# Neighbour lists without MATCH_REPLACE8, and layer 1's NaN step fused with the residual's addition

## The chip, the cores and the metric

The kernel runs on one core of one Trainium2 chip. The metric is the time of one execution on the device in microseconds (us), the median of several runs. Names of engines as in the profile: PE is TensorE, DVE is VectorE, ACT is ScalarE, POOL is GpSimd, SP is SyncE, which only starts transfers.

## The reference

Sixteen graphs of 1024 nodes with 64 features go through four layers. Every layer takes `h = relu(layernorm(x))` and adds its result to `x`. The adjacency matrix is 1024 x 1024 per graph, symmetric in where it is not zero, with some 16 neighbours per node.

```python
# layer 0: messages = adj @ h; x += tanh([h, messages] @ W1 + b1) @ W2 + b2
# layer 1:
A = edges + jnp.eye(N)
num = jnp.einsum('bij,bjd->bid', A, nodes)
denom = jnp.sum(A, axis=2, keepdims=True)
out = num / denom
x = x + jnp.where(jnp.isnan(out), 0, out)
# layer 2: thin out the neighbours of each node by rank, then, over those that remain,
adj_d = _dilate_adj(adj, mask)
agg = _weighted_nanquantile_agg(h, adj_d > 0)   # per feature: sort the neighbours' values,
                                                # 0.25*q(0.25) + 0.5*q(0.5) + 0.25*q(0.75)
x = x + (relu((h + agg) @ W1 + b1) @ W2 + b2) * mask
# layer 3: x += (adj @ h / rowsum) @ W_neighbors + h @ W_self + bias
```

Layer 2 is the dear one: for every node the values of its neighbours have to be gathered and sorted, in each of the 64 features.

## The kernel before

One program works on all graphs. Six streams (adjacency, layers, tail, gathers, lists, sorts) are Python generators; while the program is built, a simple model of the engines' clocks (`clk`) decides which stream emits its next instructions, so the order of each engine's instructions is fixed at build time. `clk.dve += 1.2` and the like are that model's durations; they do nothing on the chip but shape the order.

For layer 2, each node's row of keys is made by TensorE and ScalarE: at column j the key is 1024 - j for a neighbour that remains and 0 elsewhere, in f16. Nodes are ordered by their number of neighbours, so that 128 nodes (one per partition) with similar counts share a group. A group has a cap on the neighbours: 38, 20, 18, 16, 13, the last three for two times 128 nodes each. The lists stream gathers the rows of keys and takes the largest eight keys at a time. MAX8 finds the eight largest; MATCH_REPLACE8 (with a MATCH_VALUE_LOAD ahead of it) then puts 0 in their places, so that the next MAX8 finds the next eight:

```python
found = lists.tile([P, total], F16, name="found", bufs=1)
for b0, n, cap, _ in GROUPS:       # (0,1,38,..), (1,1,20,..), (2,2,18,..), (4,2,16,..), (6,2,13,..)
    for i in range(b0, b0 + n):
        src, at = ks[i]
        yield at
        for r in range(-(-cap // 8)):
            e = found[:, o:o + 8]
            nc.vector.max(out=e, in_=src)                                        # L1034
            clk.dve += 1.2
            if (r + 1) * 8 < cap:
                nc.vector.match_replace(out=src, in_to_replace=e, in_values=src, imm_value=0.0)  # L1037
                clk.dve += 1.3
            o += 8
            yield clk.dve
        load_keys(i + KB)          # an indirect DMA by GpSimd, L1017
index = lists.tile([P, total], I32, name="index")
ts(index, found, -1.0, float(N), op0=ALU.mult, op1=ALU.add)                      # L1043
```

GpSimd then gathers the neighbours' feature rows, one indirect DMA for each place of the list (L1154), into one buffer per group, `raw`. VectorE sorts each group with a network of minima and maxima between two buffers, `raw` and `other` (L1197), and adds up the weighted places in `agg` (L1220). `agg` goes to DRAM and comes back in the nodes' own order as `res` (L1240). A group of the next graph can be gathered only when this graph's group is sorted, as there is one `raw` per group. The node order itself is one column block `node` (L1002).

Large tensor_scalar operations elsewhere, for comparison: `gone` (L930) compares 1024 f16 values with a pointer scalar, a number per partition read from memory.

Layer 1 divides and then puts 0 for a NaN, by adding the maximum with 0 and the minimum with 0[...]. Then it adds to `x`:

```python
ts(den, p[:, :, C:C + 1], 1.0, None, op0=ALU.add)                # L1118
nc.vector.reciprocal(den, den)
o, o1 = mid(0, [P, NB, C]), mid(0, [P, NB, C])
tt(o, p[:, :, :C], ha[:, :, :C], ALU.add)                        # L1121
tt(o, o, den.to_broadcast([P, NB, C]), ALU.mult)                 # L1122
ts(o1, o, 0.0, None, op0=ALU.max)                                # L1124
ts(o, o, 0.0, None, op0=ALU.min)                                 # L1125
tt(o, o, o1, ALU.add)                                            # L1126
tt(x, x, o, ALU.add)                                             # L1127
clk.dve += 3.8
```

`ts` is tensor_scalar and `tt` tensor_tensor, both on VectorE. `den` comes from 32 matmuls of messages (L843) and ScalarE's copy of them (L844).

Of the kernel before, what the change touches and what calls it, by code (L numbers as in the profile page):

```python
# [7 lines left out]
F32 = mybir.dt.float32  # L8
F16 = mybir.dt.float16
BF = mybir.dt.bfloat16  # L10
I32 = mybir.dt.int32
U16 = mybir.dt.uint16
U8 = mybir.dt.uint8
AF = mybir.ActivationFunctionType
ALU = mybir.AluOpType
AX = mybir.AxisListType

P = 128
C = 64
NB = 8  # L20
# [10 lines left out]
B_SW, B_SW2, B_LB, B_END = 0, 252, 504, 3576  # L31
H_ID, H_OFF, H_ONE, H_G, H_PI, H_END = 0, 128, 256, 384, 516, 1028

GROUPS = [(0, 1, 38, 17), (1, 1, 20, 15), (2, 2, 18, 12), (4, 2, 16, 10), (6, 2, 13, 1)]

E_ID, E_ONE, E_CAP, E_LOW, E_CN, E_Q, E_END = 0, 128, 256, 264, 272, 280, 320
J_ID, J_BIG, J_OFF, J_ST, J_ROW, J_ONE, J_PI, J_NI, J_END = 0, 128, 256, 384, 1408, 2432, 2560, 2688, 2696
KB = 4  # L40


# [665 lines left out]
def direct_path(ctx: ExitStack, tc: tile.TileContext, t: dict, out: bass.AP, flag):  # L708
# [24 lines left out]
    identf, onesf = cf[:, E_ID:E_ID + P], cf[:, E_ONE:E_ONE + P]  # L733
    cap8, low8, cn8 = (cf[:, e:e + NB] for e in (E_CAP, E_LOW, E_CN))
    identh, big_i, offdiag = (ch[:, e:e + P] for e in (J_ID, J_BIG, J_OFF))
    stair, pidx = ch[:, J_ST:J_ST + N], ch[:, J_PI:J_PI + P]
    nid = ch[:, J_NI:J_NI + NB]
    jrow, onerow = ch[0:1, J_ROW:J_ROW + N], ch[0:1, J_ONE:J_ONE + P]
    eps = const.tile([P, 1], F32, name="eps")
# [65 lines left out]
    def mid(u, shape):  # L805

        return work.tile(shape, F32, tag=f"mid{u}", name="mid", bufs=2)
# [200 lines left out]
    def neighbour_lists(b):  # L1008


        g = state[b]
        ks = []

        def load_keys(i):
            if i < NB:
                k = lists.tile([P, N], F16, name="k", bufs=KB)
                nc.gpsimd.indirect_dma_start(k, None, g["keys_d"],  # L1017
                                             bass.IndirectOffsetOnAxis(ap=g["node"][:, i:i + 1], axis=0))
                clk.pool = max(clk.pool, clk.dve) + 1.3
                ks.append((k, clk.pool + 3.5))  # L1020

        for i in range(KB):
            load_keys(i)
        total = sum(n * -(-cap // 8) * 8 for _, n, cap, _ in GROUPS)
        found = lists.tile([P, total], F16, name="found", bufs=1)
        m = g["m"]
        o = 0
        for b0, n, cap, _ in GROUPS:
            for i in range(b0, b0 + n):
                src, at = ks[i]  # L1030
                yield at
                for r in range(-(-cap // 8)):
                    e = found[:, o:o + 8]
                    nc.vector.max(out=e, in_=src)  # L1034
                    clk.dve += 1.2
                    if (r + 1) * 8 < cap:
                        nc.vector.match_replace(out=src, in_to_replace=e, in_values=src, imm_value=0.0)  # L1037
                        clk.dve += 1.3
                    o += 8
                    yield clk.dve  # L1040
                load_keys(i + KB)
        index = lists.tile([P, total], I32, name="index")
        ts(index, found, -1.0, float(N), op0=ALU.mult, op1=ALU.add)  # L1043

        s = nodes.tile([P, 2, NB], F32, name="s")
        tt(s[:, 0], m, cap8, ALU.is_gt)
        tt(s[:, 1], m, low8, ALU.is_lt)
        tt(s[:, 0], s[:, 0], s[:, 1], ALU.max)
        tt(bad, bad, s[:, 0], ALU.max)

        at = nodes.tile([P, 3, NB], F32, name="at")
        for k in range(3):
            ts(at[:, k], m, (k + 1) / 4, -(k + 1) / 4, op0=ALU.mult, op1=ALU.add)
        far = lists.tile([P, 3, QT], F32, name="far", bufs=1)
        o = 0
        for b0, n, cap, low in GROUPS:
            lo, hi = _span(cap, low)
            k = hi + 1 - lo
            tt(far[:, :, o:o + k * n].rearrange("p t (q i) -> p t q i", i=n),
               cf[:, None, E_Q + lo:E_Q + hi + 1, None].to_broadcast([P, 3, k, n]),  # L1060
               at[:, :, None, b0:b0 + n].to_broadcast([P, 3, k, n]), ALU.subtract)
            o += k * n
        act(far, far, AF.Abs)
        for k, w in enumerate((0.25, 0.5, 0.25)):
            act(far[:, k], far[:, k], AF.Relu, bias=wcol[:, k:k + 1], scale=-w)
        g.update(index=index)
        done.add(("index", b))
        yield after(1.7, act=1.7)
        wts = lists.tile([P, QT], F32, name="wts", bufs=3)
        tt(wts, far[:, 0], far[:, 2], ALU.add)  # L1070
        tt(wts, wts, far[:, 1], ALU.add)
        clk.dve += 0.4
        g.update(wts=wts)
        done.add(("lists", b))


    def layers(b):
        g = state[b]
        adjt = g["adjt"]
        x = nodes.tile([P, NB, C], F32, name="x", bufs=3)  # L1080
        nc.sync.dma_start(x, x_in[b].rearrange("(i p) c -> p i c", p=P))
        yield max(g["at"], clk.dve + 3)
        ha = nodes.tile([P, NB, C + 1], F32, name="ha")
        yield from preln(0, x, ha)
        zt = big(0, [P, N])
        transposed(ha, zt[:C])
        messages(ha, adjt, zt[C:], C)
        tt(x, x, b02, ALU.add)
        yield after(0.7, pe=10.5, act=1.1)
        th = big(0, [C, N])  # L1090
        for q in range(2):
            p = bank()
            nc.tensor.matmul(p[:C, :], w01, zt[:, q * 512:(q + 1) * 512], start=True, stop=True)
            act(th[:, q * 512:(q + 1) * 512], p[:C, :], AF.Tanh, bias=b01)
        dh = per_node(bank(), th, w02)
        yield after(0, pe=1.3, act=2.8) + 2.8
        tt(x, x, dh, ALU.add)
        clk.dve += 0.7
        ha = nodes.tile([P, NB, C + 1], F32, name="ha")
        yield from preln(0, x, ha)  # L1100

        nc.vector.memset(ha[:, :, C:], 1.0)  # L1102
        nt = big(0, [C + 1, N])
        messages(ha, adjt, nt, 0, C + 1)
        p = bank2().rearrange("p (i m) -> p i m", m=P)
        for i in range(NB):
            nc.tensor.transpose(p[:, i, :C + 1], nt[:, i * P:(i + 1) * P], identf[:C + 1, :C + 1])

        adjt_d = dram.tile([NB, P, N], F32, name="adjt_d", bufs=5)
        deg = nodes.tile([P, 3, NB], F32, name="deg", bufs=5)  # L1110
        for j in range(NB):
            act(adjt[:, j], adjt[:, j], AF.Copy, accum_out=deg[:, 0, j:j + 1])  # L1112
            nc.sync.dma_start(adjt_d[j], adjt[:, j])
        done.add(("adjt", b))
        yield after(0, pe=10.5, act=1.1) + 2.5
        clk.act += 10
        den = nodes.tile([P, NB, 1], F32, name="den")
        ts(den, p[:, :, C:C + 1], 1.0, None, op0=ALU.add)  # L1118
        nc.vector.reciprocal(den, den)
        o, o1 = mid(0, [P, NB, C]), mid(0, [P, NB, C])  # L1120
        tt(o, p[:, :, :C], ha[:, :, :C], ALU.add)  # L1121
        tt(o, o, den.to_broadcast([P, NB, C]), ALU.mult)  # L1122

        ts(o1, o, 0.0, None, op0=ALU.max)  # L1124
        ts(o, o, 0.0, None, op0=ALU.min)  # L1125
        tt(o, o, o1, ALU.add)  # L1126
        tt(x, x, o, ALU.add)  # L1127
        clk.dve += 3.8
        ha = nodes.tile([P, NB, C + 1], F32, name="h2", bufs=3)
        yield from preln(0, x, ha)  # L1130
        nc.sync.dma_start(h_ds[b % 3][:N].rearrange("(i p) c -> p i c", p=P), ha[:, :, :C])
        ts(deg[:, 1], deg[:, 0], 0.0, None, op0=ALU.is_equal)
        tt(deg[:, 0], deg[:, 0], deg[:, 1], ALU.add)
        ts(deg[:, 1], deg[:, 1], -1.0, 1.0, op0=ALU.mult, op1=ALU.add)
        nc.vector.reciprocal(deg[:, 2], deg[:, 0])
        tt(deg[:, 2], deg[:, 2], deg[:, 1], ALU.mult)
        clk.dve += 0.6
        g.update(x=x, h2=ha, inv_deg=deg[:, 2], adjt_d=adjt_d, rows_at=clk.dve + 4)
        done.add(("layers", b))
# [226 lines left out]
def _constants():  # L1366

    import numpy as np

    p = np.arange(P)  # L1370
    ef = np.zeros((P, E_END), np.float32)
    ef[p, E_ID + p] = 1
    ef[:, E_ONE:E_ONE + P] = 1
    for b0, n, cap, low in GROUPS:
        ef[:, E_CAP + b0:E_CAP + b0 + n] = cap
        ef[:, E_LOW + b0:E_LOW + b0 + n] = low
    ef[:, E_CN:E_CN + NB] = 512 * N + N - 1 - (p[:, None] + P * np.arange(NB))
    ef[:, E_Q:E_END] = np.arange(E_END - E_Q)
    eh = np.zeros((P, J_END), np.float32)
    eh[p, J_ID + p] = 1  # L1380
    eh[p, J_BIG + p] = 2048
    eh[:, J_OFF:J_OFF + P] = 1
    eh[p, J_OFF + p] = 0
    eh[:, J_ST:J_ST + N] = p[:, None] < np.arange(N)
    eh[p, J_ST + p] = 2050
    eh[0, J_ROW:J_ROW + N] = -1024 - np.arange(N)
    eh[0, J_ONE:J_ONE + P] = 1
    eh[:, J_PI:J_PI + P] = p
    eh[:, J_NI:J_NI + NB] = p[:, None] + P * np.arange(NB)
    return {**_general_constants(), "ef": ef, "eh": eh.astype(np.float16)}  # L1390
# [73 lines left out]
```

## Time and profile before

| what | us |
|---|---|
| time, median of 3 runs | 4112.07 (4109.65 to 4116.42) |
| span of the profiled execution | 5044.8 |
| VectorE busy | 3624.5 |
| GpSimd busy | 2863.8 |
| TensorE busy, matmuls | 2152.3 |
| ScalarE busy | 1413.3 |
| MATCH_REPLACE8, 224 times | 270.7 |
| MATCH_VALUE_LOAD, 224 times | 20.6 |

The profiled execution is longer than the timed ones; sizes are read from it, and the time from the runs. In a row of the costliest groups stand the line, the engine, the operation, the output and the inputs with partitions x elements and type, then the number of instructions, the busy time in us and the mean duration of one in ns, and at the end the idle time of the engine just ahead of them with what ended it. In the view in order of time, the columns are the start in us, the duration in us, then the same.

### The profile page before, as it was taken

The numbers are of one execution on the slowest core, as the hardware profiler recorded it, in microseconds if no ns is written. First come the engines' busy times: TensorE is split into PE (matmuls) and PEld (weight loads), VectorE is DVE, ScalarE is ACT, GpSimd is POOL, SyncE is SP. The second block draws the span as 40 slices with busy tenths as digits, with TensorE's granted clock in tenths as the row PEclk, the third lists the DMA queues.
The fourth block names the chain that finished last, engine by engine and source line by source line (L and its number), as shares of the span: only waits on it lengthen the run. The fifth ranks groups of instructions, "written<-read, shape, count | busy, mean of one in ns | idle before, by whom it ended". The sixth has DMA issues, their size and how long they took to land.

```text
span 5044.8 us, 33983 instructions
## 1 busy us (share of the span) xinstructions
PE 2152.3 (43%) x8387; PEld 1001.3 (20%) x8387; DVE 3624.5 (72%) x9482; ACT 1413.3 (28%) x2594; POOL 2863.8 (57%) x2707
## 2 busy tenths in 40 slices
PE   6442414444345442454444444543445454343222
PEld 3211102121121211212121121212122121211011
DVE  2535685776678568688786868877786887768975
ACT  6332312242232421224232223323232232421000
POOL 0426366364575446756666666655676575466770
PEclk8655656666667665676666667665667666566555
DMA  3313323243242423424343343423334342333331
GB/s 107 66 60 73 62 59 52 63 98 64 77 74 63 119 35 83 66 64 111 60 105 68 97 66 87 82 56 97 70 97 74 83 81 56 79 70 78 55 55 43
DMA packets 251857, 372.70 MB, mean 74 GB/s; under 512 B 120160, under 2 KB 120352, under 8 KB 251648
## 3 DMA queue, kind: packets, MB, share of 16 engines
q0 software_dynamic: 92640, 117.88, 20.0%
q1 hardware_dynamic: 158864, 251.87, 15.1%
q8 instruction: 68, 1.11, 0.1%
q14 instruction: 141, 1.16, 0.1%
q10 hardware_dynamic: 144, 0.69, 0.0%
HBM read 256.97 MB, written 113.25 MB: 73 GB/s over the span
## 4 chain that ended last, share of the span: by engine, by line
DVE 49%; another core or an unknown queue 20%; PE 10%; issue 10%; ACT 7%; POOL 2%; DMA 2%; SPq 0%; ACTq 0%; DVEq 0%; POOLq 0%
DVE other L1197 13%; DVE raw L1197 12%; DVE found L1034 5%; DVE k L1037 4%; DVE agg L1220 4%; PE pt L843 4%; ACT adjt L1112 1%; POOL raw L1154 1%; PE pt L849 1%; DVE half L1220 1%; ACT nb L954 1%; PE tm L1284 1%; DVE nb L872 1%; ACT pt L956 1%
## 5 line engine op out<-in xcount | busy, mean ns | idle before, releaser
L1154 POOL DMA_INDIRECT raw<-h_d,index x2432 | 2554.3, 1050 | 1098.7 <-issue 722.6
L1197 DVE TENSOR_TENSOR other<-raw 128x128 f32<-128x128 f32 (+7 forms) x1488 | 763.6, 532 | 101.5 <-remote 59.4
L1197 DVE TENSOR_TENSOR raw<-other 128x256 f32<-128x256 f32 (+10 forms) x1424 | 676.5, 488 | 17.5 <-DVE other L1197 10.0
L843 PE MATMUL pt<-adjt,ha 128*65 128x512 f32 (+1 forms) x1024 | 496.5, 647 | 220.4 <-DVE ha L1102 220.3
L1017 POOL DMA_INDIRECT k<-keys_d,node x128 | 139.1, 1086 | 749.6 <-DVE node L1002 575.6
L879 PE MATMUL pt<-ef,a 128*128 128x128 f32 x1024 | 247.6, 409 | 677.3 <-ACT adjt L880 505.1
L1284 PE MATMUL tm<-at,ha 128*64 128x512 f32 x512 | 321.4, 742 | 430.2 <-issue 219.2
L954 ACT ACTIVATE nb<-pt 128x1024 f16<-128x1024 f32 x128 | 130.9, 1023 | 1123.3 <-remote 681.6
L1034 DVE MAX8 found<-k 128x8 f16<-128x1024 f16 x352 | 424.1, 1221 | 13.5 <-DVE k L1037 4.2
L920 PE MATMUL pt<-eh,nbt 128*128 128x512 f16 (+3 forms) x1024 | 221.7, 378 | 256.2 <-ACT nbt L909 157.9
L879 PEld LDWEIGHTS pt<-ef,a 128*128 128x128 f32 x1024 | 182.6, 212 | 736.4 <-ACT adjt L880 538.5
L1240 POOL DMA_INDIRECT res<-agg_d,pos x128 | 161.5, 1262 | 270.7 <-DMA agg_d<-agg 131.9
L1037 DVE MATCH_REPLACE8 k<-found,k 128x1024 f16<-128x1024 f16 x224 | 270.7, 1209 | 0.0
L843 PEld LDWEIGHTS pt<-adjt,ha 128*65 128x65 f32 (+1 forms) x1024 | 150.4, 151 | 546.3 <-issue 546.1
L1197 DVE TENSOR_TENSOR raw<-other,raw 128x128 f32<-128x128 f32 (+5 forms) x560 | 194.2, 354 | 86.2 <-remote 68.2
L1197 DVE TENSOR_TENSOR other<-raw,other 128x256 f32<-128x256 f32 (+4 forms) x592 | 206.4, 353 | 62.6 <-remote 43.3
L885 ACT ACTIVATE nb<-nb 128x512 f16<-128x512 f16 x256 | 159.5, 627 | 272.4 <-DVE nb L872 117.7
L945 PE MATMUL pt<-nb,eh 128*128 128x512 f16 x256 | 124.3, 485 | 210.3 <-ACT pt L956 132.8
L925 ACT ACTIVATE ab<-pt,sf 128x512 f16<-128x512 f32 x256 | 162.9, 693 | 175.4 <-remote 64.7
L1197 DVE TENSOR_TENSOR raw<-raw,other 128x256 f32<-128x256 f32 (+3 forms) x608 | 201.6, 336 | 0.0
L832 PE MATMUL pt<-ef,res 128*64 128x128 f32 x128 | 30.5, 418 | 393.5 <-DVE res L1244 304.3
L844 ACT COPY big<-pt 64x1024 f32<-64x1024 f32 (+1 forms) x32 | 32.2, 1008 | 583.4 <-PE pt L843 321.9
(154 smaller groups left out, 3998.9 us busy)
## 6 DMA issues: line engine op xcount, KB each, us to landing
a<-in_adj_dram SPq DMA_DIRECT2D x128, 512.0 KB
adjt_d<-adjt SPq DMA_DIRECT2D x128, 512.0 KB
at<-adjt_d SPq DMA_DIRECT2D x256, 256.0 KB
raw<-h_d,index POOLq DMA_INDIRECT x2432
keys_d<-nb SPq DMA_DIRECT2D x128, 256.0 KB
x<-in_x_dram SPq DMA_DIRECT2D x16, 256.0 KB
h_d<-h SPq DMA_DIRECT2D x16, 256.0 KB
agg_d<-agg SPq DMA_DIRECT2D x16, 256.0 KB
```

What stands on the lines that cost most here:

```text
L843: nc.tensor.matmul(p[p0:p0 + n, s], h[:, j, :n], adjt[:, j, s], start=j == 0, stop=j == NB - 1)
L879: nc.tensor.transpose(p[:, u * P:(u + 1) * P], a[:, j * P:(j + 1) * P], identf)
L920: nc.tensor.matmul(p[:, o:e], nbt[:, j, :], stair[:, :e - o], start=j % 4 == 0, stop=j % 4 == 3)
L925: act(ab[:, s], p[:, s], AF.Abs, bias=sf[:, 2 + q, i:i + 1], scale=2.0)
L954: act(nb[:, i, :], p, AF.Relu)
L1034: nc.vector.max(out=e, in_=src)
L1037: nc.vector.match_replace(out=src, in_to_replace=e, in_values=src, imm_value=0.0)
L1154: nc.gpsimd.indirect_dma_start(raw[:, s, i * C:(i + 1) * C], None, h_ds[b % 3], bass.IndirectOffsetOnAxis(ap=g["index"][:, at:at + 1], axi ...
L1197: tt(to, v0, v1, ALU.max if greater else ALU.min)
L1220: nc.vector.scalar_tensor_tensor(to, v, wq, to, op0=ALU.mult, op1=ALU.add)
L1240: nc.gpsimd.indirect_dma_start(res[:, i, :], None, g["agg_d"], bass.IndirectOffsetOnAxis(ap=g["pos"][:, i:i + 1], axis=0))
L1284: nc.tensor.matmul(p[:C, :], ha[:, j, :C], ats[k], start=j == 0, stop=j == NB - 1)
```

## The change

The lists no longer use MATCH_REPLACE8. After the first eight, the least key found so far is subtracted from every key, in place, as 16-bit whole numbers. What has been found already is then 0 or more; what has not is below 0. Read as 16-bit numbers without sign, the numbers below 0 are the largest, and the largest of them is the next key below the least. So MAX8 over that view gives the next eight, and a small tensor_scalar on eight numbers (the minimum with 0, plus the least key) makes keys of them again. In further rounds the large tensor_scalar adds the old least key and subtracts the new one in one pass. `found` is now f32[...].

Layer 1's four last operations become two: the maximum with 0 added to `x`, and the minimum with 0 added to `x`. The table `stair` has half its columns, of which the rest was not read; the model's durations are set anew.

```diff
-        found = lists.tile([P, total], F16, name="found", bufs=1)
+        found = lists.tile([P, total], F32, name="found", bufs=1)
...
-                for r in range(-(-cap // 8)):
-                    e = found[:, o:o + 8]
-                    nc.vector.max(out=e, in_=src)
-                    clk.dve += 1.2
-                    if (r + 1) * 8 < cap:
-                        nc.vector.match_replace(out=src, in_to_replace=e, in_values=src, imm_value=0.0)
-                        clk.dve += 1.3
+                nc.vector.max(out=found[:, o:o + 8], in_=src)
+                clk.dve += 1.15
+                yield clk.dve
+                less, before = src.bitcast(I16), None
+                for r in range(1, -(-cap // 8)):
+                    least = found[:, o + 7:o + 8]
+                    if r == 1:
+                        ts(less, src, least, None, op0=ALU.subtract)
+                    else:
+                        ts(less, less, before, least, op0=ALU.add, op1=ALU.subtract)
+                    before = least
+                    most = nodes.tile([P, 8], U16, name="most")
+                    nc.vector.max(out=most, in_=less.bitcast(U16))
                     o += 8
+                    ts(found[:, o:o + 8], most.bitcast(I16), 0.0, least, op0=ALU.min, op1=ALU.add)
+                    clk.dve += 1.8
                     yield clk.dve
+                o += 8
                 load_keys(i + KB)
...
-        o, o1 = mid(0, [P, NB, C]), mid(0, [P, NB, C])
+        o = mid(0, [P, NB, C])
         tt(o, p[:, :, :C], ha[:, :, :C], ALU.add)
         tt(o, o, den.to_broadcast([P, NB, C]), ALU.mult)
-        ts(o1, o, 0.0, None, op0=ALU.max)
-        ts(o, o, 0.0, None, op0=ALU.min)
-        tt(o, o, o1, ALU.add)
-        tt(x, x, o, ALU.add)
-        clk.dve += 3.8
+        nc.vector.scalar_tensor_tensor(x, o, 0.0, x, op0=ALU.max, op1=ALU.add)
+        nc.vector.scalar_tensor_tensor(x, o, 0.0, x, op0=ALU.min, op1=ALU.add)
+        clk.dve += 2.4
...
-    eh[:, J_ST:J_ST + N] = p[:, None] < np.arange(N)
+    eh[:, J_ST:J_ST + N // 2] = p[:, None] < np.arange(N // 2)
```

More of the change, by code (lines that the diff above doesn't have):

```diff
@@ L32 @@
 H_ID, H_OFF, H_ONE, H_G, H_PI, H_END = 0, 128, 256, 384, 516, 1028
+I16 = mybir.dt.int16
 GROUPS = [(0, 1, 38, 17), (1, 1, 20, 15), (2, 2, 18, 12), (4, 2, 16, 10), (6, 2, 13, 1)]
 E_ID, E_ONE, E_CAP, E_LOW, E_CN, E_Q, E_END = 0, 128, 256, 264, 272, 280, 320
-J_ID, J_BIG, J_OFF, J_ST, J_ROW, J_ONE, J_PI, J_NI, J_END = 0, 128, 256, 384, 1408, 2432, 2560, 2688, 2696
+J_ID, J_BIG, J_OFF, J_ST, J_ROW, J_ONE, J_PI, J_NI, J_END = 0, 128, 256, 384, 896, 1920, 2048, 2176, 2184
 KB = 4
@@ L735, in direct_path @@
     identh, big_i, offdiag = (ch[:, e:e + P] for e in (J_ID, J_BIG, J_OFF))
-    stair, pidx = ch[:, J_ST:J_ST + N], ch[:, J_PI:J_PI + P]
+    stair, pidx = ch[:, J_ST:J_ST + N // 2], ch[:, J_PI:J_PI + P]
     nid = ch[:, J_NI:J_NI + NB]
```

## The prediction

> **What bounds the kernel now.** I read the page's busy times first, then the chain of work that ended last, the costliest groups, the waits of GpSimd, and last the order of time inside one list phase and one layer 1. The page of the kernel before:
>
> ```profile
> PE 2152.3 (43%) x8387; PEld 1001.3 (20%) x8387; DVE 3624.5 (72%) x9482; ACT 1413.3 (28%) x2594; POOL 2863.8 (57%) x2707
> ...
> DVE 49%; another core or an unknown queue 20%; PE 10%; issue 10%; ACT 7%; POOL 2%; DMA 2%; SPq 0%; ACTq 0%; DVEq 0%; POOLq 0%
> DVE other L1197 13%; DVE raw L1197 12%; DVE found L1034 5%; DVE k L1037 4%; DVE agg L1220 4%; PE pt L843 4%; ACT adjt L1112 1%; POOL raw L1154 1%; PE pt L849 1%; DVE half L1220 1%; ACT nb L954 1%; PE tm L1284 1%; DVE nb L872 1%; ACT pt L956 1%
> ...
> L1154 POOL DMA_INDIRECT raw<-h_d,index x2432 | 2554.3, 1050 | 1098.7 <-issue 722.6
> ...
> L1034 DVE MAX8 found<-k 128x8 f16<-128x1024 f16 x352 | 424.1, 1221 | 13.5 <-DVE k L1037 4.2
> ```
>
> The profiled execution spans 5044.8 us and the timed ones 4112, 933 less. The chain has 20% (some 990 us) of waits to which no releaser is named, about the same amount. I take these waits to be mostly the profiler's own cost; that is a judgement, not shown. It matters: against 4112 us VectorE's 3624.5 us are 88%, so VectorE, which runs one fixed order of instructions, comes first. The two list lines hold 5% and 4% of the chain.
>
> GpSimd is second, and close. Its row above has 1050 ns per gather, and a pause of 722.6 us in 2370 places, 0.30 us before nearly each one. Per graph that is 152 gathers of neighbours x 1.35, 8 of `res` x (1.26 + 0.30) and 8 of `k` x (1.09 + 0.30), together 229 us. The last list of the first graph ends at 195.5 us and that of the 16th at 4617.4, 294.8 us per graph in the profile; times 4112/5044.8 that is an estimated 240 us per graph untraced. VectorE is busy 3224 us between these two, 215 per graph. So both engines are within some 10% of the period. GpSimd's waits say who leads:
>
> ```profile
> POOL k L1017 <- DVE node L1002: 575.6, 16, 120.5
> POOL raw L1154 <- DVE agg L1220: 330.3, 25, 59.7
> POOL k L1017 <- DVE found L1034: 133.3, 23, 16.0
> ```
>
> (total us, times, longest.) GpSimd waits for VectorE, for the node order, for sorted groups whose buffer it refills, and for lists; among VectorE's waits none of weight is for gathered neighbours.
>
> Now one list, in order of time (start, us, engine, line), and layer 1's end:
>
> ```profile
> 170.96 0.09 DVE L1037 MATCH_VALUE_LOAD k<-found,k 128x8 f16 x1
> 171.04 1.21 DVE L1037 MATCH_REPLACE8 k<-found,k 128x1024 f16<-128x1024 f16 x1
> 172.28 1.23 DVE L1034 MAX8 found<-k 128x8 f16<-128x1024 f16 x1
> 173.54 0.09 DVE L1037 MATCH_VALUE_LOAD k<-found,k 128x8 f16 x1
> ```
>
> ```profile
> 4000.20 0.43 DVE L1124 TENSOR_SCALAR mid<-mid 128x512 f32<-128x512 f32 x1
> 4000.66 0.43 DVE L1125 TENSOR_SCALAR mid<-mid 128x512 f32<-128x512 f32 x1
> 4001.12 0.69 DVE L1126 TENSOR_TENSOR mid<-mid 128x512 f32<-128x512 f32 x1
> 4001.84 0.70 DVE L1127 TENSOR_TENSOR x<-x,mid 128x512 f32<-128x512 f32 x1
> 4002.58 0.69 DVE L814 TENSOR_REDUCE stat<-x 128x8 f32<-128x512 f32 x1
> ```
>
> The reader is to see the pitch: 2.58 us from one round's load of match values to the next, back to back, of which the removal takes 0.08 + 1.24. Where the next instruction depends on this one, it starts some 0.03 us after its end; where it does not, 0.08 us before it.
>
> [...]tensor_scalar `gone` (L930), 1024 f16 to f16 with one pointer scalar, takes 482 ns, while MAX8 over 1024 takes 1221. [...]in the list phase 3956 to 4020 us the neighbour gathers take 946 ns, in the sort phase 4034 to 4098 they take 1158[...].
>
> **The change part by part.** Per graph there are 8 lists with 22 rounds, 14 of them after the first. Each of the 14 loses a MATCH_VALUE_LOAD and a MATCH_REPLACE8 and gains a large tensor_scalar and a small one:
>
> Before, one further round: 2.58 us.
>
> After: the large tensor_scalar as L930, 0.48, + 0.03 to its dependant; MAX8 over the unsigned view, 1.22 + 0.03, as I expect no difference by type; the small tensor_scalar on 8 elements with a pointer. For that I take `agg<-raw,wts` (L1218), 64 f32 with a pointer, 0.25, less what 56 elements cost, so 0.23, + 0.03. Together 2.02. From the second further round on the large one has two pointers. [...] So 2.08.
>
> 8 lists have a first further round (8 x 0.56) and there are 6 later ones (6 x 0.50): 4.5 + 3.0 = 7.5 us per graph, 120 us in 16 graphs.
>
> Layer 1 takes 4002.58 - 4000.20 = 2.38 us for the four operations. Two scalar_tensor_tensor over 512 f32 with two tensor inputs should cost what TENSOR_TENSOR does, 2 x (0.70 + 0.03) = 1.46. That is 0.92 less, 15 us in 16 graphs.
>
> The smaller stair table shortens one load at the start by 512 columns of f16, 128 KB, which runs beside other loads; `found` in f32 leaves the index step near its 0.25 us. Neither counts. VectorE's work falls by 135 us, 8.4 per graph.
>
> How much of it reaches the end? The chain, in its own view to a tenth of a per cent, holds (5.4 + 4.1)% x 5044.8 = 479 us of the lists' 424.1 + 270.7 + 20.6 = 715 us, two thirds; the rest lies beside layers' waits for TensorE. Two thirds of 120, and all of layer 1 since its operations follow each other, make 95 us. The instruction order of the changed program shows that with lists over sooner, sorting fills in: in several graphs `den` of layer 1 now comes after the index step with sort steps between, so the fill is not lost, and somewhat more than two thirds may arrive. I take 100 us: 4112 - 100 = 4012.
>
> **The rivals.** (a) GpSimd becomes the bound. If VectorE's 8.4 us all counted, the period would go from 240 to 232, and GpSimd needs 229[...]. Then half the gain or less arrives: about 4060. For it: the sum of 229. Against it: GpSimd still waits for VectorE in every graph, and these waits shrink when VectorE is quicker. (b) [...]a round takes 2.02 + 0.74 = 2.76 or more, 224 rounds x 0.2 = 45 us more, less layer 1's 15: about 4140. Against it: [...]the 482 ns of L930. (c) All of it arrives, as [...]sorting always stands ready (gathers of a group end more than 100 us before its sort starts): 3977. (d) The shorter lists no longer cover the messages of the layers (16 us of TensorE each, 3980 to 3996 in the trace, filled by list work alone), and a new wait before `den` takes 2 to 3 us per graph back: about 4055.
>
> **Range and chances.** The centre is between (c) and (a). 3960 to 4070 holds both and most of (d). 2% is 82 us, so faster needs three fifths of the 135 us: 0.64. Within 2%: 0.33, which is (a), (d) and (b). Slower by over 2% needs (b) with another loss: 0.03.
>
> **What would show it.** Large tensor_scalar near 0.48 (0.54 with two pointers), MAX8 unchanged at 1.22 on the unsigned view, small one near 0.23, VectorE busy some 130 us less: step one right. Gathers in the list phase staying near 0.95 us, and GpSimd still waiting for `node` and `agg`: rival (a) wrong. `den` waiting longer for TensorE: rival (d). I am wrong if the subtraction takes 1.2 us, if GpSimd is never idle any more and VectorE waits for `raw` or `k`, or if busy time falls as said and the time does not follow.

## The result: 67 us less, and GpSimd is now what VectorE waits for

The changed kernel takes 4047.34 us (median of 4 runs, 4039.05 to 4056.05), the kernel before 4114.24 (4 runs on the same chip). The ratio is 0.9836, with an interval of 0.9809 to 0.9862. The prediction was 4012, with a range of 3960 to 4070, and a chance of 0.64 that the change gains more than 2%; it gained 1.6%.

The profiled execution spans 4044.6 us, as long as the timed ones. Busy times, the chain of work that ended last by engine and by line, and the row of the neighbour gathers (busy us, mean ns, idle time before them):

```profile
PE 2039.3 (50%) x8387; PEld 980.5 (24%) x8387; DVE 3476.7 (86%) x9450; ACT 1411.8 (35%) x2594; POOL 2951.5 (73%) x2707
...
POOL 41%; DVE 33%; issue 13%; PE 5%; DMA 5%; ACT 2%; DVEq 0%; POOLq 0%; ACTq 0%
POOL raw L1165 37%; DVE other L1208 8%; DVE raw L1208 7%; DVE most L1048 5%; PE pt L845 4%; POOL res L1251 3%; DMA raw<-h_d,index 2%; DVE found L1034 2%; DVE agg L1231 2%; DVE k L1045 1%; DMA k<-keys_d,node 1%; DVE found L1050 1%; DVE k L1043 1%; ACT adjt L1125 1%; DVE nb L874 1%
...
L1165 POOL DMA_INDIRECT raw<-h_d,index x2432 | 2666.0, 1096 | 757.5 <-issue 724.7
```

GpSimd's gathers hold 37% of the chain and VectorE as a whole 33%. The instructions that replaced the removal, by form (the first two rows with one and with two pointer scalars, then MAX8 over the unsigned view, the small one, and one of layer 1's two):

```profile
L1043 DVE TENSOR_SCALAR k<-k,found 128x1024 int16<-128x1024 f16 x128 | 64.2, 502 | 3.9
L1045 DVE TENSOR_SCALAR k<-k,found 128x1024 int16<-128x1024 int16 x96 | 56.2, 585 | 2.5
L1048 DVE MAX8 most<-k 128x8 uint16<-128x1024 uint16 x224 | 275.0, 1228 | 7.7
L1050 DVE TENSOR_SCALAR found<-most,found 128x8 f32<-128x8 int16 x224 | 59.7, 267 | 8.0
L1137 DVE SCALAR_TENSOR_TENSOR x<-mid,x 128x512 f32<-128x512 f32 x16 | 11.1, 692 | 0.5
```

These are the predicted durations, nearly. GpSimd's longest waits are these (line waited for: total us, times, longest):

```profile
POOL raw L1165 <- issue: 724.7, 2378, 0.3
POOL k L1019 <- DVE node L1004: 122.0, 1, 122.0
POOL res L1251 <- DMA agg_d<-agg: 43.0, 4, 24.5
POOL res L1251 <- issue: 38.2, 120, 1.9
POOL k L1019 <- DVE found L1050: 33.9, 11, 12.7
```

The wait for `node` happens once, ahead of the first graph, and waiting for sorted groups (`agg`) has all but gone (0.6 us). What VectorE waits for in the same execution is mostly what GpSimd brings:

```profile
DVE found L1034 <- DMA k<-keys_d,node: 99.2, 13, 15.9
DVE other L1208 <- DMA raw<-h_d,index: 60.3, 8, 13.7
DVE res L1255 <- DMA res<-agg_d,pos: 52.9, 3, 32.0
```

### The profile page after: what moved, and what is told of

Its sections match the earlier page's. It is cut to its first block, busy times and chain, and to the rows that moved or that the text cites. A ratio compares the mean times of both kernels' runs of the same rounds, so it can differ in the third digit from the quotient of the medians.

```text
span 4044.6 us, 34028 instructions
## 1 busy us (share of the span) xinstructions
PE 2039.3 (50%) x8387; PEld 980.5 (24%) x8387; DVE 3476.7 (86%) x9450; ACT 1411.8 (35%) x2594; POOL 2951.5 (73%) x2707
## 4 chain that ended last, share of the span: by engine, by line
POOL 41%; DVE 33%; issue 13%; PE 5%; DMA 5%; ACT 2%; DVEq 0%; POOLq 0%; ACTq 0%
POOL raw L1165 37%; DVE other L1208 8%; DVE raw L1208 7%; DVE most L1048 5%; PE pt L845 4%; POOL res L1251 3%; DMA raw<-h_d,index 2%; DVE found L1034 2%; DVE agg L1231 2%; DVE k L1045 1%; DMA k<-keys_d,node 1%; DVE found L1050 1%; DVE k L1043 1%; ACT adjt L1125 1%; DVE nb L874 1%
## 5 line engine op out<-in xcount | busy, mean ns | idle before, releaser
L1165 POOL DMA_INDIRECT raw<-h_d,index x2432 | 2666.0, 1096 | 757.5 <-issue 724.7
L1208 DVE TENSOR_TENSOR other<-raw 128x128 f32<-128x128 f32 (+7 forms) x1488 | 766.5, 533 | 73.4 <-DMA raw<-h_d,index 60.3
L881 PE MATMUL pt<-ef,a 128*128 128x128 f32 x1024 | 232.7, 391 | 389.4 <-ACT adjt L882 354.5
L1295 PE MATMUL tm<-at,ha 128*64 128x512 f32 x512 | 286.0, 677 | 54.9 <-DMA at<-adjt_d 52.4
L1048 DVE MAX8 most<-k 128x8 uint16<-128x1024 uint16 x224 | 275.0, 1228 | 7.7
L881 PEld LDWEIGHTS pt<-ef,a 128*128 128x128 f32 x1024 | 173.5, 203 | 441.8 <-ACT adjt L882 391.0
L922 PE MATMUL pt<-eh,nbt 128*128 128x512 f16 (+3 forms) x1024 | 210.0, 364 | 125.9 <-ACT nbt L911 125.4
L1019 POOL DMA_INDIRECT k<-keys_d,node x128 | 131.0, 1023 | 191.2 <-DVE node L1004 122.0
L1034 DVE MAX8 found<-k 128x8 f32<-128x1024 f16 x128 | 156.3, 1221 | 99.2 <-DMA k<-keys_d,node 99.2
L978 ACT ACTIVATE sink<-pt,neg 128x1024 f16<-128x1024 f32 x128 | 140.4, 1121 | 244.9 <-PE pt L973 244.9
L1251 POOL DMA_INDIRECT res<-agg_d,pos x128 | 146.1, 1141 | 83.5 <-DMA agg_d<-agg 43.0
```

The lines of the kernel that those rows point to most:

```text
L881: nc.tensor.transpose(p[:, u * P:(u + 1) * P], a[:, j * P:(j + 1) * P], identf)
L922: nc.tensor.matmul(p[:, o:e], nbt[:, j, :], stair[:, :e - o], start=j % 4 == 0, stop=j % 4 == 3)
L978: act(sink, p, AF.Sign, bias=neg[:, i:i + 1], accum_out=over[:, i:i + 1])
L1034: nc.vector.max(out=found[:, o:o + 8], in_=src)
L1048: nc.vector.max(out=most, in_=less.bitcast(U16))
L1165: nc.gpsimd.indirect_dma_start(raw[:, s, i * C:(i + 1) * C], None, h_ds[b % 3], bass.IndirectOffsetOnAxis(ap=g["index"][:, at:at + 1], axi ...
```

## The experiments

**The kernel before, profiled again.** Without an edit: the profile that the prediction worked from spans 5044.8 us, and I wanted one that spans what the runs take.

> The kernel before once more, for a second profile, as the first one spanned 5045 us against 4112 timed. Theory 1 (GpSimd became the bound): span near 4112, mean gather near 1.09 us as in the changed kernel, GpSimd waiting some 5 us per graph (80 us or more in all) for sorted groups (agg) and for node, VectorE waiting under 60 us in all for gathered keys, neighbours and res (212 us in the changed kernel). Theory 2 (the shorter lists leave waits for TensorE uncovered): VectorE's waits for TensorE and ScalarE are 50 us or more below the changed kernel's 220. Theory 3 (only the new order of instructions costs): neither of the two differs by 40 us.

It took 4116.06 us in one run, and its profile spans 4114.3. So the 933 us that the prediction put down to the profiler were not the profiler's: they belong to the one execution that was profiled first. On one chip, met again below, the kernel before takes 5062 to 5174 us in every run, so the first profile looks like an execution there; where it was taken is not on record. All comparisons from here use this profile. Its busy times, chain, gathers and the waits of GpSimd for sorted groups:

```profile
PE 2057.2 (50%) x8387; PEld 978.7 (24%) x8387; DVE 3599.0 (87%) x9482; ACT 1413.4 (34%) x2594; POOL 2944.8 (72%) x2707
...
DVE 50%; POOL 20%; PE 10%; issue 8%; DMA 7%; ACT 5%; DVEq 0%; SPq 0%; POOLq 0%; ACTq 0%
...
L1154 POOL DMA_INDIRECT raw<-h_d,index x2432 | 2667.3, 1097 | 837.0 <-issue 704.7
```

```profile
POOL raw L1154 <- DVE agg L1220: 74.0, 20, 17.9
```

GpSimd held 20% of the chain already, and not 2%. It waits for `node` only 127.6 us here, 124.8 of it once, ahead of the first graph. VectorE waits 162 us for gathered keys, neighbours and `res`, against 212 with the change, so the first theory has the direction right but not its limit of 60 us; VectorE's waits for TensorE and ScalarE are 254 and 251 us, which rules the second one out. VectorE's busy time falls from 3599.0 to 3476.7, by 122 us, and the span by only 70. GpSimd's queue can be added up to its last gather (busy and idle time of its rows `raw`, `res` and `k`); what is left is the tail of the last graph. Being an account of one engine's time it proves no cause, but it shows where each microsecond went:

| us | before | changed | changed, number 3.8 | with small gaps |
|---|---|---|---|---|
| neighbour gathers, busy | 2667.3 | 2666.0 | 2628.6 | 2564.7 |
| idle before them | 837.0 | 757.5 | 757.3 | 760.5 |
| `res`, busy and idle | 211.8 | 229.6 | 216.7 | 219.5 |
| `k`, busy and idle | 327.7 | 322.2 | 323.6 | 330.2 |
| rest of the span | 70.5 | 69.3 | 70.6 | 71.4 |
| span | 4114.3 | 4044.6 | 3996.8 | 3946.3 |

(The last two columns are experiments told of below.) The change took away 80 us of idle time before gathers, of which 73 are the wait for `agg` (74.0 to 0.6), and gave 18 back at `res`.

**One part alone.** First only layer 1's part in the kernel before, with its new number for the model:

```diff
-        ts(o1, o, 0.0, None, op0=ALU.max)
-        ts(o, o, 0.0, None, op0=ALU.min)
-        tt(o, o, o1, ALU.add)
-        tt(x, x, o, ALU.add)
-        clk.dve += 3.8
+        nc.vector.scalar_tensor_tensor(x, o, 0.0, x, op0=ALU.max, op1=ALU.add)
+        nc.vector.scalar_tensor_tensor(x, o, 0.0, x, op0=ALU.min, op1=ALU.add)
+        clk.dve += 2.4
```

> Only layer 1's fusion, lists as before. VectorE does 15 us less. Theory 1: GpSimd has slack of a few us per graph in the kernel before, so nearly all arrives: 8 to 15 us less (ratio 0.996 to 0.998). Theory 2: as much. Theory 3: the order changes a little, the time moves by up to 20 us either way.

Measured: 4086.92 us against 4112.92, ratio 0.9936 (0.9921 to 0.9951), so 26 us, more than any of the three theories allowed. VectorE's busy time is 15.5 less. Then the changed kernel with the four old operations in layer 1 (the same lines of the diff the other way, number 3.8):

> Only the new lists, layer 1 as before. VectorE does some 115 us less. Theory 1: the floor set by GpSimd is reached by the lists alone, 55 to 67 us less, within 10 us of the whole change, so the two parts do not add up when the layer-1 part gives more than 10 alone. Theory 2: the whole change less layer 1's part, some 52 us less. Theory 3: time may lie anywhere between the two kernels.

Measured: 4006.24 us, ratio 0.9739 (0.9724 to 0.9753), 107 us less than before, below what each theory said. This kernel has more work for VectorE than the changed one, 3491.5 us busy instead of 3476.7, and is faster by 1%. So layer 1's part, in the presence of the lists', costs time; and as two instructions for four can hardly do that by themselves, I suspected the number 2.4, by which the model orders everything after.

**The number alone.** The changed kernel, every instruction as it is, with the old number:

```diff
-        clk.dve += 2.4
+        clk.dve += 3.8
```

> The changed kernel with one number of the build-time clock set back: layer 1's end counts 3.8 again in place of 2.4. No instruction differs, only their order, which becomes that of the lists-only kernel, the same from graph to graph. Order theory (the new order, not the fused instructions, costs the 41 us between lists-only and the whole change): 3990 to 4008 us, that is lists-only's 4006 or up to 15 less. Fusion theory (the fused instructions themselves disturb, by their waits or their reads beside the gathers): 4035 to 4055, as the changed kernel.

It ran twice, the first time in one set with three others. One has a longer number for the lists' rounds:

```diff
-                    clk.dve += 1.8
+                    clk.dve += 2.05
```

> The changed kernel with another number of the clock: a further round of a list counts 2.05 (near what it takes in the trace) in place of 1.8. Order theory: the time moves by 10 us or more, either way, though the work is the same (3990 to 4090). Fusion theory: 4047 within 10.

In the other two, the changed kernel and the one before, `res` comes by one plain transfer of SyncE instead of eight indirect ones of GpSimd; the reordering into the nodes' order is left out:

```diff
-        for i in range(NB):
-            nc.gpsimd.indirect_dma_start(res[:, i, :], None, g["agg_d"],
-                                         bass.IndirectOffsetOnAxis(ap=g["pos"][:, i:i + 1], axis=0))
-        clk.pool = max(clk.pool, clk.dve) + 10.5
-        yield clk.pool + 3.5
+        nc.sync.dma_start(res, g["agg_d"].rearrange("(i p) c -> p i c", p=P))
+        yield clk.dve + 3.5
```

> The changed kernel with res read by one plain transfer on SyncE's queue in place of 8 gathers by GpSimd, so the reordering of nodes is left out and the output is not the reference's. GpSimd loses 16 x 8 x 1.44 = 184 us of its own time, VectorE nothing. GpSimd-bound theory: the time falls by 80 us or more, to 3880 to 3965, until VectorE's 3477 busy and some 430 of its start, end and waits for TensorE hold it. VectorE- or order-bound theory: within 25 us of 4047.

> The kernel before with res read by a plain transfer in the same way. GpSimd-bound theory: the kernel before has GpSimd near its limit and VectorE just behind, so it falls by 40 to 90 us, to 4025 to 4075, and the distance between this pair (with and without the change) is the whole saving of VectorE, 100 to 135 us, not 67. If VectorE alone bound the kernel before, it stays within 20 us of 4113.

The four took 5696.36, 5386.87, 5216.43 and 5320.33 us against 5103.77 of the kernel before: that set ran on a chip where, in the first one's trace, VectorE's instructions last about as long as elsewhere (1228 ns for MAX8 over the unsigned view and 501 for the first tensor_scalar, against 1228 and 502 in the changed kernel), but which is full of waits that its repeat does not have (GpSimd waits 1074.7 us for `node`, against 128.9; 29% of the chain has no named releaser, and the weighted sums, L1231, stand 74 us idle waiting for the instruction just ahead of them on VectorE, which they do nowhere in the repeat), so these four tell nothing of where the time of the change went. There the kernel with number 3.8 is 11.8% slower than the kernel before, so what follows is not shown for such a chip. Three were repeated elsewhere; the one with the longer number for the lists was not, so what that number does stays open. First the repeat of the number 3.8:

> As the run before of the same kernel (only layer 1's number of the clock set back to 3.8), on a chip where the kernel before takes about 4113 us. Order theory: 3990 to 4008. Fusion theory: 4035 to 4055.

Measured: 4004.81 us, ratio 0.9743 (0.9729 to 0.9757). The same instructions in another order are 42 us faster than the changed kernel, and equal to the lists alone. As a check of the other direction, the lists alone with the number 2.4, whose order is that of the changed kernel apart from layer 1's own last operations:

```diff
-        clk.dve += 3.8
+        clk.dve += 2.4
```

> The lists-only kernel (layer 1's four operations as before) with the clock's number for layer 1 lowered from 3.8 to 2.4, so that it gets the changed kernel's order and none of its fused instructions. Order theory: slower than lists-only's 4006 by 25 to 60 us, 4030 to 4066, near the changed kernel's 4047. Fusion theory: 4006 within 10.

Measured: 4076.93 us against 4139.71 of the kernel before on that chip, ratio 0.9843 (0.9823 to 0.9862), where the changed kernel has 0.9836. (The range that was expected was meant for a chip on which the kernel before takes 4113 us; there the ratio makes 4048, inside it.) So the number accounts for the loss, and layer 1's two instructions for none of it. In the built order one can count the sort steps between the index steps of successive graphs. It settles at 328 with the number 3.8 (from the sixth interval on) and in the kernel before (from the eighth). With 2.4 and the new lists it goes 151, 186, 240, 405, 316, 322, 336, 332, 298, 366, 321, 335, 302, 353, 329. With 2.4 and the old lists it settles too, so it takes both new numbers to upset it. The gathers' rows of number 3.8 and of the lists alone with 2.4:

```profile
L1165 POOL DMA_INDIRECT raw<-h_d,index x2432 | 2628.6, 1081 | 757.3 <-issue 714.7
```

```profile
L1167 POOL DMA_INDIRECT raw<-h_d,index x2432 | 2683.6, 1103 | 759.2 <-issue 725.8
```

The idle time is equal; the same gathers last longer, and in the table `res` waits longer. Between the changed kernel and the one with 3.8 the span differs by 47.8 us, of which the gathers' duration is 37.4 and `res` 12.9 (20.1 more idle time, 83.5 against 63.4, and 7.2 less busy).

**Is VectorE or GpSimd the bound?** The repeats of the two kernels in which `res` is a plain transfer, the edit shown above:

> The changed kernel with res by a plain transfer (the reordering of nodes left out), on a chip where the kernel before takes about 4113 us. GpSimd-bound theory: 3880 to 3965. VectorE- or order-bound theory: within 25 us of 4047.

> The kernel before with res by a plain transfer, on a chip where it takes about 4113 us with the gathers. GpSimd-bound theory: 4025 to 4075, and 100 to 135 us above the changed kernel treated in the same way. If VectorE alone bound the kernel before: within 20 us of 4113.

Measured: 3920.57 us with the change and 4089.45 without it, against 4111.93 for the kernel before on that chip (ratios 0.9530, 0.9509 to 0.9551, and 0.9937, 0.9917 to 0.9956). The first lies in the range of the GpSimd-bound theory, the second between the two ranges. Without the change, 212 us of GpSimd's queue (`res` in the table) are worth 22. With it the time is 127 less than that of the changed kernel, but not all of that is GpSimd's work: the edit also takes the 10.5 of the eight gathers out of the model, and with that the order settles at 328 (from the ninth interval on), in spite of the number 2.4. Against the kernel with number 3.8, whose order settles too, it is 84 us (4004.81 to 3920.57), for 217 us of queue. So the same kind of work is worth a tenth of itself before the change and about two fifths after it. In the kernel before GpSimd only waits longer for VectorE instead; its waits for sorted groups, first before and then with the change, both without the reordering:

```profile
POOL raw L1154 <- DVE agg L1220: 223.3, 14, 22.9
```

```profile
POOL raw L1165 <- DVE agg L1231: 34.7, 7, 7.6
```

So VectorE led before. After the change GpSimd leads in the changed kernel (41% of the chain to VectorE's 33%). With the number 3.8 the two share it:

```profile
DVE 46%; POOL 28%; issue 10%; PE 7%; DMA 5%; ACT 4%; DVEq 0%; SPq 0%; POOLq 0%; ACTq 0%
```

The two kernels without the reordering differ by 169 us, more than the 126 us by which VectorE's busy time differs between them (3597.7 and 3472.2); I did not take that apart.

**Why gathers last longer.** A gather takes 0.945 us in the median where VectorE runs MAX8 or nothing, and more in the sorts: 1273 of the changed kernel's 2432 lie mostly beside sort steps, and these take 1.182 us in the mean. All gathers together are 368 us above 0.945. Of this 94 us are in 48 gathers of 2 us or more; with the number 3.8 it is 330 us in all, and 42 in 21 such gathers. One that begins inside a long run of sort steps, in the changed kernel, in order of time (start, us, engine, line), and VectorE's work at its end:

```profile
747.56 1.03 POOL L1165 DMA_INDIRECT raw<-h_d,index  x1 [0.30 <-issue]
748.90 5.47 POOL L1165 DMA_INDIRECT raw<-h_d,index  x1 [0.30 <-issue]
754.67 1.03 POOL L1165 DMA_INDIRECT raw<-h_d,index  x1 [0.30 <-issue]
```

```profile
752.73 0.42 DVE L1208 TENSOR_TENSOR other<-other,raw 128x256 f32<-128x256 f32 x1
753.06 0.29 DVE L1208 TENSOR_TENSOR other<-raw 128x128 f32<-128x128 f32 x1
753.26 0.29 DVE L1208 TENSOR_TENSOR other<-other,raw 128x128 f32<-128x128 f32 x1
753.59 0.42 DVE L1208 TENSOR_TENSOR other<-raw,other 128x256 f32<-128x256 f32 x1
753.93 0.42 DVE L1208 TENSOR_TENSOR raw<-other 128x256 f32<-128x256 f32 x1
```

Each step starts 0.08 us before the one ahead of it ends, as it does not depend on it, except at 753.59: that one starts 0.04 us after 753.55. It is the first such break since the gather began, and the gather ends 0.82 us after it. Of the 48 long gathers 28 end 0.60 to 0.91 us after such a break, 27 of them 0.81 to 0.83; of moments picked at random within these gathers 7% lie 0.60 to 0.91 us after one. So this gather lasts beside 18 sort steps in a row, all with two inputs, until their run has a break. That it waits for them is inferred from where such gathers end; what in it would wait is not shown.

If that is so, small breaks should cure it. The changed kernel with number 3.8, and a memset of one column, which reads nothing, after every sixth sort step:

```diff
+                steps[0] += 1
+                if steps[0] % 6 == 0:
+                    nc.vector.memset(gap, 0.0)
```

> The changed kernel with layer 1's number at 3.8, and after every sixth step of the sort networks a memset of one column on VectorE (757 in all, some 0.07 us each, 50 us), which has no SBUF input, to break the unbroken runs of two-input operations. Contention theory (a gather waits behind an unbroken run of two-input sort steps): gathers of 2 us and more, 21 in the run without memsets, fall below 8, the mean gather falls from 1.08 to 1.06 us or less, and the time is 3950 to 4005 although VectorE does more. If the gathers' length has another cause: mean gather 1.08 within 0.01 and the time 4005 to 4060.

Measured: 3941.82 us against 4139.71, ratio 0.9519 (0.9500 to 0.9537), the fastest kernel of the case that leaves nothing out, and somewhat faster than was expected. VectorE has 874 instructions more, and the program is 2.3% faster than without them (0.9519 against 0.9743, and 0.9519 / 0.9743 = 0.977). The added group, and the gathers:

```profile
L1211 DVE MEMSET gap<- 128x1 f32 x874 | 51.6, 59 | 0.0
```

```profile
L1165 POOL DMA_INDIRECT raw<-h_d,index x2432 | 2564.7, 1055 | 760.5 <-issue 714.1
```

One gather of 2 us or more is left, and all gathers together are 63.9 us shorter than with number 3.8. The span is 50.5 shorter, though on a chip where the kernel before takes 0.7% longer; by the ratios the gain is some 92 us, so not all of it is accounted for. Most of the lengthening stays: 266 us of 330 above 0.945. At the place shown above the gathers now take (the same columns):

```profile
747.83 0.98 POOL L1165 DMA_INDIRECT raw<-h_d,index  x1 [0.30 <-issue]
749.12 0.94 POOL L1165 DMA_INDIRECT raw<-h_d,index  x1 [0.30 <-issue]
750.36 1.11 POOL L1165 DMA_INDIRECT raw<-h_d,index  x1 [0.30 <-issue]
```

At the memset of this place VectorE shows no idle time, but one sort step starts 0.26 us after the one ahead instead of 0.20 (first with the memset, then the same two steps in the changed kernel):

```profile
749.11 0.33 DVE L1208 TENSOR_TENSOR raw<-other 128x128 f32<-128x128 f32 x1
749.37 0.41 DVE L1208 TENSOR_TENSOR raw<-raw,other 128x256 f32<-128x256 f32 x1
749.39 0.06 DVE L1211 MEMSET gap<- 128x1 f32 x1
```

```profile
749.64 0.28 DVE L1208 TENSOR_TENSOR raw<-other 128x128 f32<-128x128 f32 x1
749.84 0.42 DVE L1208 TENSOR_TENSOR raw<-raw,other 128x256 f32<-128x256 f32 x1
```

That the gathers use these places can be counted. Of the 291 gathers that still take 1.2 us or more, 52 end 0.80 to 0.83 us after the end of a memset, where 0.4% of moments picked at random within them lie, and 140 as long after a break of the run (1.7%). The program became shorter with its gathers while VectorE's busy time rose from 3475.0 to 3484.7 us, so the gathers' length was on its path. How often the memset is best placed was not tried.

## Why the prediction held, and where its steps were off

**VectorE's saving: right.** 135 us predicted, 122 measured. The terms that were off are small: the later rounds' large tensor_scalar takes 585 ns and not 540 (it has a second pointer, but also a second operation and another input type than the first one with its 502, so the pointer's own share is not shown), and the small tensor_scalar takes 267 ns and not 230. MAX8 on the unsigned view is as fast as before, 1228 ns where it took 1221 on f16. The subtraction to 16-bit whole numbers is as fast, nearly, as `gone` on f16: 1024 results in 502 ns, against 496 for `gone` in the same execution. So rival (b), in which it takes MAX8's 1.22 us, is out. Why `found` is f32 is not shown: no run leaves it f16. Layer 1's part saves 15.5 us of busy time in the experiment, 15 predicted.

**What of it arrives: the path was wrong, and the number in the range all the same.** "Two thirds of 120, and all of layer 1" made 100 us; 67 came. The sum takes VectorE as the engine that leads, with its shares read from the chain of a profile 933 us too long, in which GpSimd had 2%. In the profile that fits the runs GpSimd has 20% before the change, and 41% after it. The sign that the prediction gave for itself being wrong came: GpSimd hardly waits for VectorE any more, and VectorE waits for `k` (99.2 us) and `raw` (60.3). The range held because it was drawn wide enough for rival (a), at "about 4060", and the outcome with the chance of 0.64 did not come. That the number 3.8 gives 107 us with the same instructions, close to the 100, is luck: layer 1's part adds nothing there (ratios 0.9739 without, 0.9743 with it), and alone, in the kernel before, it gave 26, which is more than its 15. Both stay open.

**The term that was missing: the order.** The prediction looked at the instruction order only for whether lists' savings are filled with sorting. That a new number for layer 1 makes the order irregular, with 48 gathers of 2 us or more in place of 21 and `res` later, costs 42 us (4047.34 against 4004.81), and was not in the sum.

**Rival (a), GpSimd becomes the bound: this is what happened.** The 229 us per graph were about right: busy 2943.1 and issue 788.8 in its three rows are 233 per graph. What I held against it, that GpSimd waits for VectorE in every graph, was read from the disturbed profile; its waits for sorted groups were 74.0 us in all, and the change used them up. That the new 16-bit tensor_scalar holds gathers up is not seen: gathers that lie mostly beside it take 0.953 us in the mean (74 of them). Those mostly beside sort steps, which were there before, take 1.182.

**Rival (c), all arrives: no**, 67 us of 122. **Rival (d), waits before `den`: no**, 49.7 us before and 38.7 after.

**The judgement on the 20% of waits without a releaser: wrong.** I took them for the profiler's cost and said so. The kernel before has none in its chain when its profile spans 4114.3 us, and where they appeared again, in the first run of the number 3.8, the profiled execution was as long as the timed ones (5697.97 us, median 5696.36).

## What to carry to other kernels

When two engines stand within some per cent of one another, the time that the second waits for the first gives a rough measure of what a saving on the first is worth: add up these waits in a profile that is as long as the timed runs before working out a gain. Here they were 74 us and 67 came. It is no ceiling: in an order in which the second engine's own gathers were also 39 us shorter, 107 came. In a program whose order comes from a model, change a duration in the model as an experiment of its own, since it can cost as much as the instructions save. And where GpSimd gathers beside long runs of independent two-input VectorE instructions, try a tiny instruction without inputs every few steps, and count the long gathers before and after: here those of 2 us or more went from 21 to one.

## What was not expected of the hardware

- A gather that takes 0.945 us in the median beside MAX8 or an idle VectorE takes up to 5.47 us in the changed kernel beside back-to-back TENSOR_TENSOR steps with two inputs, and 27 of its 48 gathers of 2 us or more end 0.81 to 0.83 us after a break of them. A 59 ns memset in every sixth place leaves one of 21 such gathers, and takes 64 of 330 us off what all gathers take above 0.945 us. That the gather waits for these steps is inferred, and what in it would wait is not shown.
- A tensor_scalar over 1024 elements of 16 bits takes 502 ns with one pointer scalar and one operation (f16 to int16), 585 with two of each (int16 to int16).
